# A recommender's phase change reordered: exponent and gates ahead of copies, block tests on GpSimd, late sums shared anew, one step's attention weights by TensorE

## The chip, the cores and the metric

The kernel runs on one core of one Trainium2 chip. The metric is the device time of one execution in microseconds (us). Before the change it is 1994.08 us, the median of 3 runs (1992.85 to 1997.23). The engines are named as the profile names them: PE is TensorE (PEld its weight loads), DVE is VectorE, ACT is ScalarE, POOL is GpSimd, and SP issues most of the DMAs.

## The reference, cut to what matters

For 1024 samples with a history of 100 steps and 128 features, in float32:

```python
# first recurrence (GRU) over the history
r, z = sigmoid(...), sigmoid(...)
n = tanh(i_n + r * h_n)
h = (1 - z) * n + z * h                     # keys[t] = h
# attention scores: an MLP over [keys, q, keys - q, q * keys]; softmax over the 100 steps
attn = softmax(where(mask == 1, score, -inf))
pooled = einsum('bt,btd->bd', attn, keys)   # 1024 x 128
att_seq = pooled.T[:T]                      # step t of the next recurrence uses feature t of pooled
# second recurrence over the keys, from h = 0
r, u = sigmoid([h, x_t] @ Wr.T + br), sigmoid([h, x_t] @ Wu.T + bu)
h_hat = tanh([h * r, x_t] @ Wh.T + bh)
u = att_seq[t][:, None] * u
h = (1 - u) * h + u * h_hat
# the state at the sample's last step, and four other features, go through a last MLP
```

Two things matter here. The weight of step t is column t of `pooled`, so the second recurrence can only begin when the softmax over all 100 steps and the sums over the last keys are done. And the second recurrence runs on samples sorted by length, so that fewer and fewer columns stay alive.

## The kernel before

The 1024 samples stand as two halves of 512 columns, with 128 features on the partitions. `gru_phase` runs the first recurrence: in each of 100 turns TensorE computes both halves' gates and, for the step before, the score MLP (`attend` issues its products, `take` its relus and sends the score rows through a DMA into tiles called s_b). A softmax runs in blocks of 8 to 3 steps: `late_scores` and `late_tops` on VectorE bring the scores into place and take off their maximum, `exponents` runs on ScalarE, and `late_sums` finishes the weights. `Half.pool` multiplies keys by weights and adds them into `pooled`: L713 rescales the old sum, L723 multiplies, L724 adds. `augru_phase` runs the second recurrence.

Everything is issued in an order that is written by hand; each engine takes its own instructions strictly in that order and waits by semaphores. There is no scheduler.

The change is in the passage between the two phases, from `take(T - 2)` to the first steps of `augru_phase`. What stands there before the change:

- `features(g)`: eight groups of four products that begin the last MLP, each into one of two PSUM banks (called f); ScalarE copies each group out (L774), and only then is a bank free for the group after next.
- `where_equal`: an equality test on ScalarE, made of Square (L1083) and Relu (L1084). Four such tests are needed: two on the tiles called block, two on the halves of q0.
- `gate` and `activate`: step 0 of the second recurrence, which has no old state: two products for each half (L1136) and a tanh and a sigmoid for each (L1143).
- The weights of steps 0 to 3 are computed apart from the rest, since the phase needs them first: VectorE sums the first four features (the slice `soon`) of all keys (L733, L1174, L1177) into first_w (L1181); TensorE brings these into the sorted order (L1193), VectorE masks them with block into s_b (L1195), and TensorE adds up groups of partitions (L1198 for step 0, L1208 for a row of each of the four steps). The four rows go through DRAM (att_d) and come back spread over all partitions, by one load for each half and step (L1221 for steps 1 and 2).
- The late sums: the other 28 features (the slice `rest`) of the last seven keys. GpSimd sums all of half 0's last but one block, then half 1's; VectorE sums half 0's last block, one key between the products of step 0, the rest behind them.
- `store_pooled` writes `pooled` to DRAM by eight stores (L1230); `gather_weights` fetches it back in sorted order by eight indirect DMAs of GpSimd (L165); VectorE masks it (L1272) and TensorE transposes it (L1279) in step 2 and 3, for the weights of steps 4 to 99.

PSUM has eight banks. In the passage six of them are the tiles `b[0]` to `b[5]`, shared out by the dictionary `banks` among softmax (e), score transposes (pt), sums (kw) and features (f); `LATE_BANKS` and `NEXT_BANKS` say which of them the first gates of the second phase take, in the order in which they come free.

## Time and profile before

| | before |
|---|---|
| median of 3 runs | 1994.08 us (1992.85 to 1997.23) |
| the profiled execution | 1990.86 us |
| its span, first to last instruction | 1989.1 us |
| ScalarE busy, 1390 to 1400 us | 6.98 of 10 us |
| VectorE busy, 1400 to 1410 us | 5.99 of 10 us |
| GpSimd busy, 1400 to 1410 us | 9.61 of 10 us |
| TensorE's idle time between 1430 and 1440 us | 1.05 us |

A row of an engine's timeline has its start and its length in us, the engine, the line of the kernel, the operation, output and inputs, their shapes and the count of instructions merged into it. In square brackets stands how long the engine had been idle just before, and what released it. The chain of work that ended last goes back from the last instruction to whatever released it, step by step. The times of the timeline are counted from the start of the span; the score MLP's last products end at about 1389 us, and the second phase's own gates begin at 1410.69.

### The profile page before, as it was taken

The page shows a single profiled execution, that of the slowest core. Times are in us where ns is not written, and L with a number is a line of the kernel's source. Part 1 is how long each engine was busy: PE and PEld are TensorE (multiplying, and loading weights), DVE is VectorE, ACT ScalarE, POOL GpSimd, SP SyncE. Part 2 cuts the span into 40 slices and gives each one's busy share as a digit, 9 for nine tenths or more (in the row PEclk, how much of TensorE's full clock was granted, in tenths as well). Part 3 has the DMA queues.
Part 4 walks back from the last instruction along what each step waited for, and adds up shares of the span by engine and source line. Part 5 has one row for each costly group of instructions (what it writes and reads, how often), then busy time and mean ns, then how long its engine had stood idle before and what let it go on. Part 6 is the DMA issues. An engine that isn't in the chain of part 4 may idle for free.

```text
span 1989.1 us, 40757 instructions
## 1 busy us (share of the span) xinstructions
PE 1969.7 (99%) x15252; PEld 919.1 (46%) x15252; DVE 1667.6 (84%) x3010; ACT 935.8 (47%) x1681; POOL 1241.9 (62%) x1283
## 2 busy tenths in 40 slices
PE   9999999999999999999999999999899999999998
PEld 2333333333333333333333333443444556678997
DVE  7888899898979898888889888998677778888995
ACT  4444454454544444444445454445343444445553
POOL 1324759676896959588795948797653454445331
PEclk9999999999999999999999999999999999999999
DMA  4453333223333434356743333332543333333331
GB/s 116 109 111 105 104 107 101 88 86 108 117 100 116 117 101 116 106 152 188 210 151 98 102 104 97 108 96 94 161 139 92 96 111 96 93 103 99 83 82 33
DMA packets 245171, 218.57 MB, mean 110 GB/s; under 512 B 45639, under 2 KB 206900, under 8 KB 244196
## 3 DMA queue, kind: packets, MB, share of 16 engines
q1 hardware_dynamic: 233476, 183.30, 33.0%
q0 software_dynamic: 11200, 32.04, 5.6%
q8 instruction: 122, 2.00, 0.4%
q14 instruction: 85, 0.70, 0.1%
q10 hardware_dynamic: 288, 0.52, 0.1%
HBM read 153.45 MB, written 60.72 MB: 108 GB/s over the span
## 4 chain that ended last, share of the span: by engine, by line
PE 94%; DVE 2%; POOL 1%; DMA 1%; ACT 1%; issue 1%; SPq 0%; another core or an unknown queue 0%; DVEq 0%; ACTq 0%; POOLq 0%
PE ps L612 50%; PE pm L798 17%; PE ph L1329 4%; PE pu L1329 4%; PE pr L1329 4%; PE pr L1325 4%; PE pu L1325 4%; PE ph L1325 4%; POOL pooled L724 1%; POOL kw L723 1%; PE pr L1405 0%; PE ph L1405 0%; DMA item<-att_d 0%; SPq L1230 0%; PE p L1527 0%
## 5 line engine op out<-in xcount | busy, mean ns | idle before, releaser
L612 PE MATMUL ps<-x,wih 128*32 128x512 f32 x4800 | 834.9, 593 | 0.0
L612 PE MATMUL ps<-hn,whh 128*32 128x512 f32 x4752 | 829.0, 592 | 0.0
L612 PEld LDWEIGHTS ps<-x,wih 128*32 128x32 f32 x4800 | 237.2, 110 | 324.4 <-issue 311.6
L612 PEld LDWEIGHTS ps<-hn,whh 128*32 128x32 f32 x4752 | 235.2, 110 | 320.2 <-issue 312.4
L624 ACT ACTIVATE r<-ps,brz 128x512 f32<-128x512 f32 x200 | 137.6, 688 | 380.2 <-PE ps L612 379.9
L597 POOL TENSOR_TENSOR xm<-x,m 128x512 f32<-128x512 f32 x200 | 234.3, 1172 | 83.6 <-DMA m<-mask_d 83.2
L798 PE MATMUL pm<-kq,wkq 128*32 128x512 f32 x1188 | 270.0, 592 | 0.0
L798 PE MATMUL pm<-hn,wk 128*32 128x512 f32 x1188 | 269.9, 592 | 0.0
L598 POOL TENSOR_TENSOR hist<-hist,xm 128x512 f32<-128x512 f32 x200 | 258.9, 1295 | 15.7
L724 POOL TENSOR_TENSOR pooled<-pooled,kw 128x512 f32<-128x512 f32 (+1 forms) x195 | 250.3, 1284 | 15.3
L798 PE MATMUL pm<-mv,w 128*32 128x512 f32 x790 | 252.7, 592 | 2.9 <-DVE e L939 2.9
L723 POOL TENSOR_TENSOR kw<-kt,e 128x512 f32<-128x512 f32 (+1 forms) x195 | 210.0, 1077 | 71.7 <-DVE e L956 71.7
L645 ACT ACTIVATE ps<-ps,bih 128x512 f32<-128x512 f32 x198 | 131.1, 662 | 224.9 <-DVE ps L642 224.0
L208 POOL DMA_INDIRECT rows<-keys_d,idx_k x186 | 182.1, 979 | 73.3 <-POOL rows L207 70.0
L1337 ACT ACTIVATE c<-ph,bh 128x510 f32<-128x510 f32 (+57 forms) x174 | 88.3, 507 | 252.7 <-PE ph L1329 252.6
L632 DVE SCALAR_TENSOR_TENSOR u<-ps,bhh,r 128x512 f32<-128x512 f32 x198 | 147.5, 745 | 69.7 <-PE ps L612 63.9
L655 DVE TENSOR_TENSOR d<-hn,ps 128x512 f32<-128x512 f32 x198 | 136.1, 687 | 36.0 <-ACT ps L645 35.7
L207 POOL COPY rows<-rest 128x1 f32<-128x1 f32 x186 | 35.3, 190 | 199.5 <-DVE rest L1365 177.2
L656 DVE TENSOR_TENSOR d<-ps,d 128x512 f32<-128x512 f32 x198 | 136.9, 691 | 27.0 <-ACT ps L646 12.8
L664 ACT COPY hn<-ps 128x512 f32<-128x512 f32 x198 | 115.4, 583 | 91.8 <-DVE kq L659 91.8
L642 DVE TENSOR_TENSOR ps<-ps,u 128x512 f32<-128x512 f32 x200 | 140.0, 700 | 21.9 <-PE ps L612 0.9
L1357 DVE TENSOR_TENSOR pu<-pu,c 128x510 f32<-128x510 f32 (+57 forms) x173 | 81.9, 473 | 75.0 <-ACT c L1337 72.8
(286 smaller groups left out, 3154.3 us busy)
## 6 DMA issues: line engine op xcount, KB each, us to landing
x<-in_hist_x SPq DMA_DIRECT2D x210, 256.0 KB
keys_d<-kt SPq DMA_DIRECT2D x44, 1024.0 KB
m<-mask_d SPq DMA_DIRECT2D x200, 128.0 KB
wide_d<-kt SPq DMA_DIRECT2D x24, 256.0 KB
sorted_d<-sort SPq DMA_DIRECT2D x32, 192.0 KB
rows<-sorted_d SPq DMA_DIRECT2D x6, 1024.0 KB
s_b<-mv SPq DMA_DIRECT2D x200, 8.0 KB
rows<-keys_d,idx_k POOLq DMA_INDIRECT x186, 2.9
```

The costliest lines, as they stand in the source:

```text
L208: nc.gpsimd.indirect_dma_start(out=r[:, k, :], out_offset=None, in_=keys_d[q], in_offset=bass.IndirectOffsetOnAxis(ap=idx_k[:, k, i : i + ...
L597: nc.gpsimd.tensor_mul(d, x, m)
L598: nc.gpsimd.tensor_add(acc, acc, d)
L612: nc.tensor.matmul(p[ts(q, R), :], lhsT=w[:, g, ts(q, R)], rhs=v, start=(j == 0), stop=(j == len(parts) - 1),)
L624: nc.scalar.activation(r, pr, AF.Sigmoid, bias=brz[:, 0:1])
L632: nc.vector.scalar_tensor_tensor(out=u, in0=ph, scalar=bhh[:, 2:3], in1=r, op0=ALU.add, op1=ALU.mult,)
L642: nc.vector.tensor_add(pi, pi, u)
L723: eng.tensor_mul(d, k, w)
L724: eng.tensor_add(acc, acc, d)
L798: nc.tensor.matmul(p[i][s, :], lhsT=w[:, s], rhs=v, start=start, stop=stop)
L1325: nc.tensor.matmul(p, lhsT=m[:, 1, :], rhs=k, start=True, stop=False)
L1329: nc.tensor.matmul(p, lhsT=m[:, 0, :], rhs=v, start=False, stop=True)
```

## The change

- ScalarE's tests of block (two of the four) become one GpSimd instruction each (add and is_equal, L1104 of the changed kernel), ahead of the sums.
- Features 3 go ahead of half 0's gates; the test of half 0's q0 and the tanh follow; the exponent goes ahead of the copies of features 4 to 7, and half 1's gates go into the banks of pt, ahead of features 6 and 7 instead of behind them.
- Of half 1's last but one block VectorE now sums the rescale and two keys of `rest`, ahead of the last block's scores; GpSimd keeps two. In exchange GpSimd takes two of the three keys of half 0's last block; VectorE keeps one, now behind step 0's products.
- The first sums go into a PSUM tile (first_sums) and are copied to `pooled` afterwards; first_w reads them there.
- Step 0's two products of state and update move from ahead of the maskings to between them.
- The weight of step 1 for half 0 comes from a product of TensorE (at1) instead of a load; the load for half 0 is gone. The sigmoid of that step's update gate goes to SBUF (into item).
- `store_pooled` stores half 1 first. The banks change places.

The order of the instructions on three engines. **TensorE**, behind the last products of the score MLP (pm), before the change; ph and pu are half 0's gates of step 0, `last` the bank of features:

```order
L798 MATMUL pm<-mv,w_0_135 32x512
L798 MATMUL pm<-mv,w_late 32x512
L1136 MATMUL ph<-h_all,wh 128x512
L1136 MATMUL pu<-h_all,wu 128x512
L766 MATMUL last<-m_9180,user 128x200
```

And with the change:

```order
L798 MATMUL pm<-mv,w_0_135 32x512
L798 MATMUL pm<-mv,w_late 32x512
L766 MATMUL last<-m_9180,user 128x200
L766 MATMUL last<-m_9180,item 128x200
L766 MATMUL last<-m_9180,hist 128x200
L766 MATMUL last<-m_9180,cross 128x200
L1143 MATMUL ph<-h_all,wh 128x512
L1143 MATMUL pu<-h_all,wu 128x512
```

One group of features now stands between the score MLP's last products and the gates that reuse its banks.

**ScalarE**, from the second relu of the last scores (mv) on, before the change; L953 is the exponent, L774 a copy of features, L1143 a gate's tanh or sigmoid:

```order
L865 ACTIVATE mv<-pm,bm_147 32x512
L1083 ACTIVATE block<-block,low 128x512
L1084 ACTIVATE block<-block 128x512
L774 COPY part<-last 128x200
L1143 ACTIVATE h_all<-ph,bh 128x512
L774 COPY part<-last 128x200
L1083 ACTIVATE q_160<-q_160,low 128x512
L1084 ACTIVATE q_160<-q_160 128x512
L953 ACTIVATE last<-last 128x32x4
L1156 ACT_TABLE_LOAD
L1156 ACTIVATE table<-table 128x1
L1143 ACTIVATE pu<-pu,bu 128x512
```

And with the change (L1150 is now the tanh or sigmoid):

```order
L865 ACTIVATE mv<-pm,bm_147 32x512
L774 COPY part<-last 128x200
L1083 ACTIVATE q_160<-q_160,low 128x512
L1084 ACTIVATE q_160<-q_160 128x512
L1150 ACTIVATE h_all<-ph,bh 128x512
L1083 ACTIVATE q_160<-q_160,low 128x512
L1084 ACTIVATE q_160<-q_160 128x512
L953 ACTIVATE last<-last 128x32x4
L774 COPY part<-last 128x200
L1163 ACT_TABLE_LOAD
L1163 ACTIVATE table<-table 128x1
L1150 ACTIVATE pu<-pu,bu 128x512
```

The test of block is gone, both tests of q0 stand ahead of the exponent, and a copy stands behind it.

**VectorE**, from first_w to the late sums, before the change:

```order
L1181 TENSOR_TENSOR first_w<-pooled,used 128x128
L975 COPY e<-last 128x32x5
L1189 TENSOR_TENSOR h_all<-h_all,pu 128x512
L1189 TENSOR_TENSOR h_all<-h_all,last 128x512
L713 TENSOR_TENSOR pooled<-pooled,last 128x16x28
L723 TENSOR_TENSOR last<-kt,last 128x16x28
L724 TENSOR_TENSOR pooled<-pooled,last 128x16x28
L1195 TENSOR_TENSOR s_b_156<-last,block 128x512
L1195 TENSOR_TENSOR s_b_158<-last,block 128x512
L1205 TENSOR_TENSOR h_all<-first,h_all 128x512 x2
```

And with the change:

```order
L1189 TENSOR_TENSOR first_w<-last,used 128x128
L975 COPY e<-last 128x32x5
L1193 COPY pooled<-last 128x32x4
L1199 TENSOR_TENSOR h_all<-h_all,pu 128x512
L1201 TENSOR_TENSOR s_b_156<-last,block 128x512
L1199 TENSOR_TENSOR h_all<-h_all,last 128x512
L1201 TENSOR_TENSOR s_b_158<-last,block 128x512
L1211 TENSOR_TENSOR h_all<-first,h_all 128x512 x2
L713 TENSOR_TENSOR pooled<-pooled,last 128x16x28
L723 TENSOR_TENSOR last<-kt,last 128x16x28
L724 TENSOR_TENSOR pooled<-pooled,last 128x16x28
```

The late sums of half 0 move behind step 0's products, and each s_b follows its own half's product.

The diff:

```diff
@@ -75,7 +75,7 @@
 WIDTHS = [[max(LEAST, n) for n in alive] for alive in ALIVE]
 
 FREE = 134 * 256
-LATE_BANKS, NEXT_BANKS = (1, 0, 5), (2, 6, 3, 4)
+LATE_BANKS, NEXT_BANKS = (2, 0, 1), (6, 5, 3, 4)
 
 PR = P // NH
 BQ = B // (P // R)
@@ -1099,7 +1099,9 @@
         take(T - 2)
         halves[1].keep()
         nc.scalar.activation(table, table, AF.Exp)
-        where_equal(later["block", 0], low[:, 1:2])
+        for half in halves:
+            block = later["block", half.i]
+            nc.gpsimd.tensor_scalar(block, block, low[:, 1:2], 0.0, ALU.add, ALU.is_equal)
         some(0)
         attend(T - 1, [b[0], b[1]])
         for half in halves:
@@ -1121,12 +1123,17 @@
         halves[0].pool(T, nc.gpsimd)
         late_1 = list(halves[1].todo)
         halves[1].pool(T, nc.vector, soon)
+        halves[1].todo = late_1
+        halves[1].pool(2, nc.vector, rest)
+        halves[1].pool(T, nc.gpsimd, rest)
         attend(T)
         take(T)
         some(2)
         attend(T + 1)
         some(2)
         take(T + 1)
+        some(3)
+        some(3)
         for half in halves:
             half.store((T - 1) // G)
         gates = []
@@ -1144,24 +1151,24 @@
             return to
 
         gate(halves[0], [pa.tile([P, HB], F32, tag="a", name=f"p{n}") for n in "hu"])
-        where_equal(later["block", 1], low[:, 1:2])
-        some(3)
-        some(3)
+        where_equal(q0[:, ts(0, HB)], low[:, 0:1])
         activate()
         some(4)
-        some(4)
-        where_equal(q0[:, ts(0, HB)], low[:, 0:1])
+        where_equal(q0[:, ts(1, HB)], low[:, 0:1])
         stage(2)
         exponents()
+        some(4)
+        some(5)
+        gate(halves[1], banks["pt"])
         nc.scalar.activation(table, table, AF.Sigmoid)
         update = [activate()]
-        for g in range(5, 2 * GH):
-            some(g)
-            some(g)
-        where_equal(q0[:, ts(1, HB)], low[:, 0:1])
-        gate(halves[1], banks["f"])
+        some(6)
+        some(5)
         activate()
         update.append(activate())
+        some(7)
+        some(6)
+        some(7)
 
         stage()
         e = soft["e"][1]
@@ -1174,23 +1181,22 @@
         nc.vector.tensor_mul(
             d[:, :, 0], pooled[:, :, soon], e[:, :, 0:1].to_broadcast([P, NK, SOON])
         )
+        first_sums = b[0][:, HB - NK * SOON :].rearrange("p (k c) -> p k c", c=SOON)
         nc.vector.tensor_reduce(
-            pooled[:, :, soon], d.rearrange("p k n c -> p k c n"), AX.X, ALU.add
+            first_sums, d.rearrange("p k n c -> p k c n"), AX.X, ALU.add
         )
         w = wp.tile([P, HB], F32, tag="d", name="first_w")[:, : SOON * NK]
         nc.vector.tensor_mul(
-            w.rearrange("p (k c) -> p k c", c=SOON), pooled[:, :, soon], later["used"]
+            w.rearrange("p (k c) -> p k c", c=SOON), first_sums, later["used"]
         )
         weights_to_sbuf()
-        halves[1].todo = late_1 + halves[1].todo
+        nc.vector.tensor_copy(pooled[:, :, soon], first_sums)
         halves[1].pool(T, nc.gpsimd, rest)
 
-        for i in range(NH):
-            nc.vector.tensor_mul(h3[i], h3[i], update[i])
-        halves[0].pool(1, nc.vector, rest)
-        chosen = []
-        for half, p in zip(halves, banks["pt"]):
+        later["chosen"] = chosen = []
+        for half, p in zip(halves, (b[3], b[2])):
             nc.tensor.matmul(p, lhsT=w, rhs=q0[:, half.cols], start=True, stop=True)
+            nc.vector.tensor_mul(h3[half.i], h3[half.i], update[half.i])
             chosen.append(s_bs[NH * (soft["j"] % 2) + half.i])
             nc.vector.tensor_mul(chosen[-1], p, later["block", half.i])
         for half in halves:
@@ -1203,7 +1209,7 @@
                 stop=True,
             )
             nc.vector.tensor_mul(h3[half.i], p, h3[half.i])
-        p = banks["pt"][0]
+        p = b[3]
         for half in halves:
             nc.tensor.matmul(
                 p[ts(half.i, R), :], lhsT=quad, rhs=chosen[half.i], start=True, stop=True
@@ -1215,16 +1221,17 @@
                 out=att_d[i][:SOON], in_=soon_rows[i * R : i * R + SOON, :]
             )
         for t in range(1, 3):
-            for half in halves:
+            for half in halves[2 - t :]:
                 at = item[:, half.cols] if t == 1 else s_bs[NH * ((soft["j"] - 1) % 2) + half.i]
                 later["att", t, half.i] = at
                 nc.sync.dma_start(out=at, in_=att_d[half.i][t].partition_broadcast(P))
-        halves[0].pool(T, nc.vector, rest)
+        halves[0].pool(1, nc.vector, rest)
+        halves[0].pool(T, nc.gpsimd, rest)
         later["halves"] = halves
 
     def store_pooled():
 
-        for half in later["halves"]:
+        for half in reversed(later["halves"]):
             to = pooled_d[half.cols, :].rearrange("(k r) f -> r k f", r=R)
             for p in range(P // R):
                 nc.sync.dma_start(
@@ -1348,10 +1355,22 @@
             if (t, i) == (1, 0):
                 open_gates(1, 0, ("pu",), LATE_BANKS[1:])
             pu = close_gate(t, i, "pu", wu, h)
+            if (t, i) == (1, 0):
+                att[1, 0] = pa.tile([P, HB], F32, tag="a", name="at1")
+                nc.tensor.matmul(
+                    att[1, 0],
+                    lhsT=quad[:, 1:2].to_broadcast([P, P]),
+                    rhs=later["chosen"][0],
+                    start=True,
+                    stop=True,
+                )
             if t == 1:
                 open_gates(1, i, ("ph",), (None, LATE_BANKS[2])[1 - i :])
             nc.scalar.activation(pr, pr, AF.Sigmoid, bias=later["br"])
-            nc.scalar.activation(pu, pu, AF.Sigmoid, bias=later["bu"])
+            u = item[:, :w] if (t, i) == (1, 0) else pu
+            nc.scalar.activation(u, pu, AF.Sigmoid, bias=later["bu"])
+            if (t, i) == (1, 0):
+                pu = att[t, i][:, :w]
             state = states.pop(1 - i, None)
             if state is not None:
                 nc.vector.tensor_mul(state[0], state[0], state[1])
@@ -1359,7 +1378,7 @@
             nc.vector.tensor_mul(r, h, pr)
             if state is not None:
                 nc.vector.tensor_sub(state[3], state[0], state[2])
-            nc.vector.tensor_mul(pu, pu, att.pop((t, i))[:, :w])
+            nc.vector.tensor_mul(pu, u, att.pop((t, i))[:, :w])
             rest = wp.tile([P, HB], F32, name="rest")[:, :w]
 
             nc.vector.scalar_tensor_tensor(
@@ -1607,7 +1626,7 @@
             for i in range(NH):
                 keys[t, i] = later["key", t, i]
                 if t < G - 1:
-                    att[t, i] = later["att", t, i]
+                    att[t, i] = later.get(("att", t, i))
                 else:
                     load_att(t, i)
         open_gates(1, 0, ("pr",), LATE_BANKS)
```

## The prediction

> **What bounds the kernel now.** I read the page first, then the busy time by stretch, then the engines in order of time between 1378 and 1434 us (all instants are us from the start of the span).
>
> ```profile
> span 1989.1 us, 40757 instructions
> PE 1969.7 (99%) x15252; PEld 919.1 (46%) x15252; DVE 1667.6 (84%) x3010; ACT 935.8 (47%) x1681; POOL 1241.9 (62%) x1283
> ...
> 1390.00:1400.00 10.00, 8.52 (x44) 7.25 (x44) 5.63 (x16) 6.98 (x14) 9.69 (x10) 1.00 0.80 233
> 1400.00:1410.00 10.00, 7.34 (x16) 2.79 (x16) 5.99 (x11) 2.82 (x5) 9.61 (x10) 0.83 0.19 62
> 1405.90:1409.20 3.30, 2.80 (x4) 1.17 (x4) 1.73 (x3) 0.00 (x0) 3.14 (x4) 0.50 0.00 0
> 1440.00:1950.00 510.00, 509.37 (x2094) 355.41 (x2094) 421.92 (x1022) 244.46 (x539) 234.01 (x399) 1.00 0.37 99
> ```
>
> TensorE is busy for 99% of the span, so the kernel is as long as TensorE's queue plus TensorE's stops. The columns of the stretches are: length, busy PE, PEld, DVE, ACT, POOL, granted clock, DMA. The phase change is the weak place: between 1390 and 1410 TensorE is idle for 4.1 us, and from 1405.9 to 1409.2 its granted clock is 0.50. Behind it the second phase is full again (509.37 of 510), so what is won here goes through to the end. TensorE's own rows name the stops:
>
> ```profile
> 1389.81 1.12 PE L1136 MATMUL ph<-h_all,wh 128*128 128x512 f32 x2 [0.76 <-ACT mv L865]
> 1391.63 0.50 PE L766 MATMUL last<-m,user 128*128 128x200 f32 x2
> 1392.99 0.50 PE L766 MATMUL last<-m,user 128*128 128x200 f32 x2
> 1398.68 0.61 PE L766 MATMUL last<-m,user 128*128 128x200 f32 x2 [1.48 <-ACT part L774]
> 1401.00 1.02 PE L1136 MATMUL last<-h_all,wu 128*128 128x512 f32 x2
> 1401.86 1.88 PE L1193 MATMUL last<-q,first_w 128*128 128x512 f32 x4
> 1406.40 3.38 PE L1198 MATMUL first<-s_b,quad 128*128 128x512 f32 x4 [2.66 <-DVE s_b L1195]
> 1409.71 1.05 PE L1208 MATMUL last<-s_b,quad 128*32 128x512 f32 x4
> 1433.84 0.64 PE L1279 MATMUL pw<-ident,att_r 128*96 128x128 f32 x4 [0.63 <-DVE att_r L1272]
> ```
>
> Three stops: 0.76, 1.48 and 2.66 us. One group of features takes 1392.99 - 1391.63 = 1.36 us, one 128x512 product 1401.86 - 1401.00 = 0.86. The two products of L1198 (four records) should take 1.72 and took 1409.71 - 1406.40 = 3.31: **1.59 us lost to the half clock** that followed the longest stop. The stop of 1.48 left the clock at 1.00. Together 0.76 + 1.48 + 2.66 + 1.59 = 6.49 us are to be had.
>
> [...]
>
> **The change, part by part.** *Stop 1.* Features 3 now stand ahead of half 0's gates. ScalarE's relus (below) end as before, and 1.36 us of products cover the 0.76. Won: 0.76.
>
> *Stop 2 and the exponent.* ScalarE's rows of before:
>
> ```profile
> 1389.08 1.38 ACT L865 ACTIVATE mv<-pm,bm 32x512 f32<-32x512 f32 x2 [0.65 <-PE pm L798]
> 1394.76 0.72 ACT L1083 ACTIVATE q<-q,low 128x512 f32<-128x512 f32 x1
> 1396.06 0.26 ACT L953 ACTIVATE last<-last 128x128 f32<-128x128 f32 x1
> 1396.33 1.28 ACT L1156 ACT_TABLE_LOAD   x1
> 1398.31 0.55 ACT L774 COPY part<-last 128x200 f32<-128x200 f32 x2
> ```
>
> An equality test costs 1396.06 - 1394.76 = 1.30 here. Two of the four leave for GpSimd, and the exponent moves ahead. From 1390.46 on (the end of the two relus) ScalarE now has a copy (0.3, half of the 0.55), a test, a tanh (0.7, as one of the two relus) and a test: 1390.46 + 0.3 + 1.3 + 0.7 + 1.3 = 1394.1. VectorE decides when the exponent can start:
>
> ```profile
> 1388.82 0.18 DVE L899 COPY last<-top 128x32 f32<-128x32 f32 x1
> 1391.69 1.47 DVE L905 STREAM_TRANSPOSE last<-s_b 128x512 f32<-128x512 f32 x2 [2.69 <-DMA s_b<-mv]
> 1393.86 0.30 DVE L912 TENSOR_TENSOR last<-last,top 128x128 f32<-128x128 f32 x1
> 1396.35 0.27 DVE L920 TENSOR_TENSOR last<-last,on 128x96 f32<-128x96 f32 x1 [2.19 <-ACT last L953]
> 1398.79 0.30 DVE L1174 TENSOR_TENSOR last<-pooled,last 128x128 f32<-128x128 f32 x1
> 1399.84 0.86 DVE L1181 TENSOR_TENSOR first_w<-pooled,used 128x128 f32<-128x128 f32 x1
> 1403.94 0.61 DVE L713 TENSOR_TENSOR pooled<-pooled,last 128x448 f32<-128x448 f32 x1
> 1405.66 1.28 DVE L1195 TENSOR_TENSOR s_b<-last,block 128x512 f32<-128x512 f32 x2
> 1410.42 0.62 DVE L723 TENSOR_TENSOR last<-kt,last 128x448 f32<-128x448 f32 x1
> 1411.73 0.63 DVE L723 TENSOR_TENSOR last<-kt,last 128x448 f32<-128x448 f32 x1
> ```
>
> Into the wait of 2.69 us the change puts half 1's rescale and two of its late sums: 1405.66 - 1403.94 = 1.72 with one sum, 1411.73 - 1410.42 = 1.31 for the second, 3.03 in all. They run from 1388.8 to 1391.85, so the transposes start at 1392.0, 0.3 later. The scores, less their maximum, are ready at 1394.16 + 0.3 = 1394.5; the exponent starts then instead of at 1396.06. ScalarE's copies that release TensorE's banks follow at once, or 2.3 us later behind table load, sigmoid and copy (about 1397.3). TensorE, without its stops, stands at 1389.05 + 1.36 + 1.72 + 2.72 + 1.72 = 1396.6 when it wants the first bank and at 1397.9 for the second. Won: 1.48.
>
> *Stop 3 and the clock.* The sum of step 0's weights waits for GpSimd's four sums of half 0:
>
> ```profile
> 1386.90 1.07 POOL L713 TENSOR_TENSOR pooled<-pooled,e 128x512 f32<-128x512 f32 x1 [6.27 <-DVE e L975]
> 1397.45 0.97 POOL L713 TENSOR_TENSOR pooled<-pooled,e 128x448 f32<-128x448 f32 x1
> 1407.12 0.97 POOL L713 TENSOR_TENSOR pooled<-pooled,e 128x448 f32<-128x448 f32 x1
> 1413.37 1.15 POOL L724 TENSOR_TENSOR pooled<-pooled,kw 128x448 f32<-128x448 f32 x1
> L1583 POOL TENSOR_SCALAR places<-places,own 128x256 f32<-128x256 f32 x1 | 0.9, 941 | 0.1
> ```
>
> After the exponent, VectorE comes to the product of L1174 at 1394.8 + (1398.79 - 1396.35) = 1397.24, and half 0's sums end by 1397.45, when the next piece starts: a wait of some 0.2 us, on the edge. first_w starts 1.05 later (1399.84 - 1398.79), at 1398.5. Its price was 0.86; the same size from PSUM (L1174) took 0.30. It now reads its sums from PSUM, so I take 0.30 (ends 1398.8) and keep 0.86 (1399.4) as the other end. [...] TensorE reaches this point at 1389.05 + 5 x 1.36 + 4 x 0.86 = 1399.3, so it waits for at most 0.1. Its two products end at 1401.0. VectorE meanwhile has two small copies (0.3 each by L1174's size) and then, for each half, one product and one s_b, 0.64 each (half of 1.28), with no late sums (1.72) among them: from 1399.4 on, s_b of half 0 is ready at 1400.7, of half 1 at 1402.0. TensorE's first product of L1198's kind runs from 1401.0 to 1401.9 and the second waits for 0.1 to 0.6, by first_w's price; I take 0.3. A stop of that length keeps the clock. Won: 2.66 + 1.59 - 0.3 = 3.95.
>
> *Block tests on GpSimd.* Two tests of 512 columns; 256 columns took 0.94 with one operation, so 0.94 to 1.9 each, from below, and I take 1.9 (twice the columns). Two are 3.8 us and lie in the 6.27 us in which GpSimd waited: cost nothing, up to 3.1 us each.
>
> *Step 1 by TensorE.* One more 128x512 product in TensorE's dense part: 0.86, in full. It spares one broadcast load and VectorE's wait for it, which had not stopped TensorE.
>
> *Late sums, stores, gather.* Behind stop 3, the next thing that TensorE can wait for is the transpose of the gathered weights at 1433.84:
>
> ```profile
> 1432.42 0.69 DVE L1365 SCALAR_TENSOR_TENSOR rest<-pu,h_all 128x506 f32<-128x506 f32 x1
> 1433.22 0.56 DVE L1272 TENSOR_TENSOR att_r<-att_r,used_s 128x384 f32<-128x384 f32 x1
> ...
> 1415.83 7.66 SPq L1230 DMA_DIRECT2D pooled_d<-pooled  x8
> ...
> 1413.49 4.78 DMA item<-att_d
> 1429.74 3.36 DMA att_r<-pooled_d,idx
> ```
>
> GpSimd had 1397.45 - 1386.90 = 10.55 (half 0), 1407.12 - 1397.45 = 9.67 and 1414.52 - 1407.12 = 7.40 (half 1) us of sums; the rescale and two of the four sums of the middle piece go to VectorE, and two sums of half 0's last piece come instead (4.4), so it ends at 1413.6, 0.9 before its 1414.52. What counts is SP: the eight stores stood behind six broadcast loads (1413.49, 4.78 us), though the sums were done at 1414.52. The loads now come 6.2 us earlier and are five; half 1's stores can go at 1409.3 and only half 0's four wait for 1413.6. At 0.5 to 0.7 each they are out by 1416.2 instead of 1423.5: 7 us earlier, and the gather with them. TensorE gets there 6.2 - 0.86 = 5.3 earlier, so the gather (landed at 1433.10, just before VectorE's mask) keeps ahead by some 1.5 us. Of the stop of 0.63 about 0.1 goes, since the mask still stands behind VectorE's rest.
>
> **The sum.** 0.76 + 1.48 + 3.95 - 0.86 + 0.1 = 5.4 us won. The profiled execution took 1990.86 (span 1989.1 and 1.8 around it), which would become 1985.4. The median of the three runs shown is 1994.08, 3.2 above the profiled one; on that scale the forecast is 1994.08 - 5.4 = **1988.7**. About 0.2% (4.0 us) is what a measurement of this kernel can tell from no change, so the forecast is only just outside it.
>
> **Rivals.** *The gather becomes the wait* (chance 0.13). If the eight stores still take 7.66 us from the moment the last sum is done, they end at 1421.3, 2.2 earlier than before; TensorE then stands at the transpose for 3.1 us more, and a stop of that length halved the clock before. Won: 2.2, or 0.6 with another 1.59 lost: 1991.9 to 1993.5. For it: the last piece of sums ends only 0.9 us earlier. Against it: the slow issues stood beside loads that now end earlier.
>
> *VectorE's new sums hold the exponent* (0.09). If the two sums placed at 1388.8 cost what GpSimd's do (0.97 + 2 x 2.2 = 5.4 instead of 3.03), scores, exponent and first_w are 2.4 later; TensorE idles for 1.9. Won: 3.5, or 1.9 if the clock falls: 1990.6 to 1992.2. Against it: the same instructions, from PSUM, are in the rows above.
>
> *Slower: the block tests hold GpSimd* (0.04). Half 0's sums start when the tests end, and the sum of step 0's weights already waits for them on the edge, so each us over 6.27 is a us of TensorE, and from about 2.5 us on the half clock is back. It decides from 4.2 us over, 5.2 us a test. At 7.5 a test it is 8.7 over: 8.7 - 0.4 + 1.59 - 5.4 = 4.5 slower, 1998.6. For it: no test of this size on GpSimd is in the trace. Against it: 0.94 for half the columns.
>
> *More is won* (0.06): first_w at 0.30 and no stop left, 6.3 us, 1987.8.
>
> **How the numbers follow.** The forecast has 0.68. Its own range is 1986.7 to 1990.7, two us to each side, about half the spread of the three runs before (1992.85 to 1997.23). Taking in the gather and the held exponent gives 1985.5 to 1992.8 with some 2 in 10 outside. A win of 5.4 shows as over 0.2% in about five of six measurements: 0.68 x 0.83 + 0.06 + a little of the held exponent = 0.64 faster; slower 0.05 from the block tests and chance; 0.31 within 0.2%.
>
> **What would show it.** Right: no row of TensorE between 1389 and 1405 with more than 0.5 us of idling, granted clock 1.00 throughout, the products of L1198's kind at 0.86 each; the exponent on ScalarE near 1394.5; first_w near 0.30; both block tests done by 1386.9; the products that follow them on TensorE near 1403.5 (1409.71 before); the last store issued near 1416. Wrong: a wait of several us before the transposes of the gathered weights, GpSimd's first sum of half 0 later than 1387, or the clock at 0.50 anywhere in this stretch.

## The result and the profile after

| | before | after |
|---|---|---|
| median of 7 runs each, side by side | 1994.55 us (1992.85 to 1997.23) | 1988.49 us (1985.91 to 1990.21) |
| the profiled execution | 1990.86 us | 1985.99 us |
| its span | 1989.1 us | 1984.2 us |
| ScalarE busy, 1390 to 1400 us | 6.98 of 10 us | 7.48 |
| VectorE busy, 1400 to 1410 us | 5.99 of 10 us | 6.16 |

The changed kernel is faster: after to before 0.9967 (95% interval 0.9955 to 0.9978), 6.06 us by the medians and 4.87 us by the two profiled executions.

From the page after and from its busy time by stretch, with the columns of the prediction (length, busy PE, PEld, DVE, ACT, POOL, granted clock, DMA share, GB/s):

```profile
span 1984.2 us, 40759 instructions
PE 1969.6 (99%) x15254; PEld 921.9 (46%) x15254; DVE 1667.0 (84%) x3012; ACT 932.7 (47%) x1677; POOL 1242.7 (63%) x1284
...
1390.00:1400.00 10.00, 10.00 (x44) 7.25 (x43) 8.18 (x24) 7.48 (x15) 9.61 (x10) 1.00 0.92 266
1400.00:1410.00 10.00, 9.93 (x24) 3.76 (x25) 6.16 (x10) 1.92 (x3) 9.61 (x10) 1.00 0.34 104
1440.00:1950.00 510.00, 507.52 (x2103) 355.59 (x2102) 420.36 (x1027) 242.90 (x540) 230.01 (x393) 1.00 0.36 98
```

TensorE's 4.1 idle us between 1390 and 1410 have shrunk to 0.07, and the clock stays at 1.00. But the second phase, 509.37 busy us of 510 before, now shows 507.52: something was lost behind the stretch that the change is about, and the experiments have to say whether the change lost it.

TensorE's own rows after, from the timeline (start, length, engine, line, operation, shapes; the idle time ahead in square brackets). L1198 is the product with first_w, L1204 the sum for step 0, L1214 the rows for the four steps, L1360 the new product of step 1, L1286 the transposes pw:

```profile
1398.07 1.88 PE L1198 MATMUL last<-q,first_w 128*128 128x512 f32 x4
1399.87 2.32 PE L1204 MATMUL first<-s_b,quad 128*128 128x512 f32 x4
1402.13 1.05 PE L1214 MATMUL last<-s_b,quad 128*32 128x512 f32 x4
...
1406.64 1.02 PE L1360 MATMUL at<-s_b,quad 128*128 128x512 f32 x2
...
1426.90 0.64 PE L1286 MATMUL pw<-ident,att_r 128*96 128x128 f32 x4 [0.42 <-DVE att_r L1279]
1433.16 0.61 PE L1286 MATMUL pw<-ident,att_r 128*96 128x128 f32 x4 [0.51 <-PE pu L1332]
```

No row between the score MLP and pw carries a wait any more. One wait is hidden in a merged row: the four records of L1204 take 2.26 us to the start of the next row, the four of L1198 ahead of them 1.80.

The rows of ScalarE's exponent, VectorE's first_w and GpSimd's first gather after:

```profile
1393.03 0.26 ACT L953 ACTIVATE last<-last 128x128 f32<-128x128 f32 x1
1397.36 0.29 DVE L1189 TENSOR_TENSOR first_w<-last,used 128x128 f32<-128x128 f32 x1
1417.35 1.05 POOL L165 DMA_INDIRECT att_r<-pooled_d,idx  x1 [5.05 <-DMA pooled_d<-pooled]
```

The instants of two executions can't be compared as they stand, since the first 1378 us differ by up to 2 us from run to run (the copy below starts between 1377.87 and 1379.82 in the fourteen profiles). I therefore count from VectorE's copy L899, the last one ahead of all that was changed, in each trace:

```profile
1377.87 0.18 DVE L899 COPY last<-top 128x32 f32<-128x32 f32 x1
```

It started at 1379.09 in the profile before. **The stretch from L899 to the first pw** was 1433.84 - 1379.09 = 54.75 us and is 1426.90 - 1377.87 = 49.03 us: 5.72 us won. Where it was won, by starts of TensorE's rows, in us after L899:

| TensorE's row | before | after | won in this piece |
|---|---|---|---|
| product with first_w | 22.77 | 20.20 | 2.57 |
| first sum for step 0 | 27.31 | 22.00 | 2.74 |
| rows of the four steps | 30.62 | 24.26 | 1.05 |
| pw | 54.75 | 49.03 | -0.64 |

The last piece holds the new product of step 1 (0.86 us more) and a shorter wait at pw (0.63 before, 0.42 after).

In the one repeat of the changed kernel (last experiment) these starts came out within 0.1 us, so single steps of 0.3 us and more can be judged by them, where medians with a spread of 4 us cannot.

### The profile page after: what moved, and what is told of

It reads as the page before. It is cut to its first block, busy times and chain, and to the rows that moved or that the text cites. A ratio compares the mean times of both kernels' runs of the same rounds, so it can differ in the third digit from the quotient of the medians.

```text
span 1984.2 us, 40759 instructions
## 1 busy us (share of the span) xinstructions
PE 1969.6 (99%) x15254; PEld 921.9 (46%) x15254; DVE 1667.0 (84%) x3012; ACT 932.7 (47%) x1677; POOL 1242.7 (63%) x1284
## 4 chain that ended last, share of the span: by engine, by line
PE 95%; DVE 3%; issue 1%; ACT 1%; DVEq 0%; ACTq 0%
PE ps L612 50%; PE pm L798 17%; PE ph L1336 4%; PE pr L1336 4%; PE pu L1336 4%; PE pr L1332 4%; PE pu L1332 4%; PE ph L1332 4%; PE last L766 1%; PE pr L1424 0%; PE ph L1424 0%; DVE pu L1381 0%; DVE ps L657 0%; DVE d L656 0%; DVE pu L1376 0%
## 5 line engine op out<-in xcount | busy, mean ns | idle before, releaser
L612 PE MATMUL ps<-x,wih 128*32 128x512 f32 x4800 | 812.5, 592 | 0.0
L612 PE MATMUL ps<-hn,whh 128*32 128x512 f32 x4752 | 806.9, 592 | 0.0
L798 PE MATMUL pm<-hn,wk 128*32 128x512 f32 x1188 | 264.4, 592 | 0.0
L798 PE MATMUL pm<-kq,wkq 128*32 128x512 f32 x1188 | 264.4, 592 | 0.0
L798 PE MATMUL pm<-mv,w 128*32 128x512 f32 x790 | 247.4, 593 | 2.0 <-DVE e L939 2.0
L657 DVE TENSOR_TENSOR ps<-ps,d 128x512 f32<-128x512 f32 x198 | 138.5, 699 | 6.7
```

The lines of the kernel that those rows point to most:

```text
L612: nc.tensor.matmul(p[ts(q, R), :], lhsT=w[:, g, ts(q, R)], rhs=v, start=(j == 0), stop=(j == len(parts) - 1),)
L657: nc.vector.tensor_add(pi, pi, d)
L798: nc.tensor.matmul(p[i][s, :], lhsT=w[:, s], rhs=v, start=start, stop=stop)
```

## The experiments

My theory: the win is TensorE's three stops and the half clock, less the new product, and the gather keeps ahead. The rivals are those of the prediction: the gather hard behind, the exponent, GpSimd's tests. Each kernel below is the changed one with one part undone, except the first, which is the kernel before with one thing added. The measure is the stretch from L899 to pw, 49.03 us in the changed kernel.

| kernel | L899 to pw, us | against the changed kernel |
|---|---|---|
| before | 54.75 | +5.72 |
| before_filler | 53.12 | +4.09 |
| order_before | 51.62 | +2.59 |
| features_behind | 49.84 | +0.81 |
| sums_ahead | 50.24 | +1.21 |
| tests_act | 49.48 | +0.45 |
| tests_x3 | 56.39 | +7.36 |
| sums_sbuf | 49.73 | +0.70 |
| sums_shared_before | 49.11 | +0.08 |
| stores_before | 49.52 | +0.49 |
| step1_load | 48.17 | -0.86 |
| pair_and_load | 49.14 | +0.11 |
| after_again | 49.10 | +0.07 |

**The half clock by itself** (before_filler): the kernel before, and TensorE kept busy through its longest stop.

```diff
             nc.vector.tensor_mul(chosen[-1], p, later["block", half.i])
+        for _ in range(3):
+            nc.tensor.matmul(
+                b[2], lhsT=later["wh"][:, 1, :], rhs=q0[:, :HB], start=True, stop=True
+            )
```

> The kernel before, with three products of 512 columns (3 x 0.86 = 2.58 us, into a bank that nobody reads) where TensorE stopped for 2.66 us. They start when the weights' products end, so the next products can start when they did. If the half clock is the price of that stop: the granted clock stays at 1.00, the four records of L1198's kind take 1.72 instead of 3.31 us, and the stretch from VectorE's copy L899 (the last before 1380 us) to the first transposes pw takes 54.75 - 1.6 = 53.15 us. Rival, the clock falls for another reason (the load of the whole passage): still 0.50 there, stretch 54.75. Rival, the gather follows hard behind: clock at 1.00, but 1 us or more of new waiting at pw, stretch 54.2 or more.

TensorE's rows of this kernel (L1197 the filler, L1202 and L1212 the sums that were L1198 and L1208; `<-issue` stands where the profile shows nothing that was waited for):

```profile
1402.56 2.74 PE L1197 MATMUL last<-q,wh 128*128 128x512 f32 x6
1405.38 1.98 PE L1202 MATMUL first<-s_b,quad 128*128 128x512 f32 x4
1407.30 1.05 PE L1212 MATMUL last<-s_b,quad 128*32 128x512 f32 x4
...
1431.22 0.64 PE L1283 MATMUL pw<-ident,att_r 128*96 128x128 f32 x4 [0.42 <-issue]
```

The sums start when they did (27.28 us after L899, 27.31 before), but their four records take 1407.30 - 1405.38 = 1.92 us instead of 3.31, and 1.63 us of the stretch are gone, with useless work. So 1.4 us of the win is the clock alone; the other 0.2 is the idle time at pw, 0.42 instead of 0.63.

Two stretches of 1 us of the kernel before (the columns again) give the same size in another way:

```profile
1405.00:1406.00 1.00, 0.00 (x0) 0.00 (x0) 0.97 (x3) 0.00 (x0) 0.92 (x2) 0.92 0.00 0
1409.00:1410.00 1.00, 1.00 (x4) 0.14 (x4) 0.39 (x2) 0.00 (x0) 0.92 (x2) 0.88 0.00 0
```

Mean clocks of 0.92 and 0.88 put the half clock from about 1405.84 to 1409.24, 3.4 us. TensorE worked from 1406.40 on, and half of the 2.84 us up to 1409.24 is 1.42. The record has one profile of the kernel before; whether its clock falls here in every execution is not shown.

**The order of gates, copies and exponent** (order_before): the passage between the last scores and the last sums as before, without block's test.

```diff
-        some(3)
-        some(3)
...
         gate(halves[0], [pa.tile([P, HB], F32, tag="a", name=f"p{n}") for n in "hu"])
-        where_equal(q0[:, ts(0, HB)], low[:, 0:1])
+        some(3)
+        some(3)
         activate()
         some(4)
-        where_equal(q0[:, ts(1, HB)], low[:, 0:1])
+        some(4)
+        where_equal(q0[:, ts(0, HB)], low[:, 0:1])
         stage(2)
         exponents()
...
-        gate(halves[1], banks["pt"])
+        gate(halves[1], banks["f"])
```

> The changed kernel with gates, copies of features, q0's tests and the exponent in the order of before (block tests on GpSimd, the sums, s_b and step 1's product stay as changed). ScalarE's copies wait for TensorE's features there, so the exponent starts 17.0 us after L899 again (15.2 in the changed kernel), and two stops of TensorE come back, 0.76 and 1.48 us; what follows is as in the changed kernel. Stretch from L899 to pw 49.03 + 2.2 to 2.6 = 51.3 to 51.6 us, the clock stays at 1.00. Rival, the exponent is early without the new order, since a test of block is gone from ScalarE: only the 0.76 returns, 49.8 us. Rival, the stops of before add up to a half clock here: 53 us.

```profile
1389.88 1.13 PE L1141 MATMUL ph<-h_all,wh 128*128 128x512 f32 x2 [0.72 <-ACT mv L865]
...
1396.77 0.50 PE L766 MATMUL last<-m,cross 128*128 128x200 f32 x2
1398.75 0.61 PE L766 MATMUL last<-m,user 128*128 128x200 f32 x2 [1.48 <-ACT part L774]
1399.19 0.50 PE L766 MATMUL last<-m,item 128*128 128x200 f32 x2
```

Both stops return, with the exponent 17.0 us after L899 again, though a test is gone from ScalarE: TensorE's features, not ScalarE's load, set it in that order. These TensorE rows also show why a stop costs more than its brackets. Rows of this kind start 0.34 us apart in the dense parts. Around the stop they start 1398.75 - 1396.77 = 1.98 apart, and the next 1399.19 - 1398.75 = 0.44: 1.74 us lost, where the brackets say 1.48. Of the 0.26 between, 0.16 is the row's own length (the brackets count from the end of a row, 0.50 us after its start, and dense rows start 0.34 apart), and 0.10 is the slower first row behind the stop.

**Stop 1 alone** (features_behind): features 3 behind half 0's gates, their copy behind the tanh.

```diff
-        some(3)
-        some(3)
...
+        some(3)
         where_equal(q0[:, ts(0, HB)], low[:, 0:1])
         activate()
+        some(3)
```

> The changed kernel with features 3 behind half 0's gates again, their copy behind the tanh. TensorE stops for 0.76 us ahead of the gates. The exponent comes 0.4 us later, which lies in VectorE's wait of 0.62 us for GpSimd's sums. Stretch 49.03 + 0.76 = 49.8 us. Rival, the stop is absorbed by a later wait (the 0.46 us between the two sums of step 0's weights): 49.3 us.

0.81 us, as expected; the wait was not absorbed later. The exponent starts 15.60 us after L899, 0.44 later than in the changed kernel, and VectorE's wait for GpSimd falls from 0.62 to 0.21: that lateness was hidden as expected.

**VectorE's late sum ahead of s_b** (sums_ahead).

```diff
+        halves[0].pool(1, nc.vector, rest)
         later["chosen"] = chosen = []
...
-        halves[0].pool(1, nc.vector, rest)
         halves[0].pool(T, nc.gpsimd, rest)
```

> The changed kernel with VectorE's one late sum of half 0 (rescale, product, sum: about 1.9 us) ahead of s_b, as it stood before. VectorE idles for 0.46 us there, so s_b comes some 1.4 us later and TensorE stops for that before it adds up groups of partitions. If the clock falls by the stop's length, 1.4 to 1.9 us leave it at 1.00, as the 1.48 us of before did: stretch from L899 to pw 49.03 + 1.4 to 1.9 = 50.4 to 50.9 us. Rival, any stop at this place halves the clock: 52.0 us or more.

```profile
1402.06 2.32 PE L1205 MATMUL first<-s_b,quad 128*128 128x512 f32 x4 [1.09 <-DVE s_b L1202]
1404.31 1.05 PE L1215 MATMUL last<-s_b,quad 128*32 128x512 f32 x4
```

The stop is 1.09 us, where I had expected 1.4 to 1.9; the stretch is 1.21 us longer, and the granted clock stays at 1.00 (1400 to 1408 us): the four records take 2.25 us as in the changed kernel. So the rival, that any stop at this place halves the clock, does not hold in this run. That the length decides is not shown either (last experiment).

The late sum gives back 1.09 us of stop 3, not 2.66. In the kernel before, VectorE did something else ahead of s_b:

```profile
1403.33 0.69 DVE L1189 TENSOR_TENSOR h_all<-h_all,last 128x512 f32<-128x512 f32 x1 [1.80 <-ACT last L1143]
```

It waited 1.80 us for ScalarE's last gate of half 1, for a product that the first s_b did not need. With the change that gate comes earlier and the product stands behind the first s_b. No run put the product back in front, so this share of the win is read from the rows and not tested.

**Block's tests** (tests_act, tests_x3): back on ScalarE; and three times on GpSimd.

```diff
-        for half in halves:
-            block = later["block", half.i]
-            nc.gpsimd.tensor_scalar(block, block, low[:, 1:2], 0.0, ALU.add, ALU.is_equal)
+        where_equal(later["block", 0], low[:, 1:2])
...
+        where_equal(later["block", 1], low[:, 1:2])
         where_equal(q0[:, ts(0, HB)], low[:, 0:1])
```

> The changed kernel with the two tests of block back on ScalarE, the first where it was before, the second ahead of q0's first test. ScalarE and VectorE are both ready for the exponent at 1393.0 in the changed kernel, so a test of 1.3 us more makes the exponent 1.3 us later; 0.6 of it lies in VectorE's wait for GpSimd's sums, and TensorE has 0.4 to spare: stretch from L899 to pw 49.03 + 0.3 to 0.9 = 49.3 to 49.9 us. Rival, the tests' place is what the new order hangs on (the copies that release TensorE's banks come late too): 50.3 us or more. Rival, ScalarE had the time: 49.0 us.

```diff
             block = later["block", half.i]
+            for _ in range(2):
+                spare = wp.tile([P, HB], F32, tag="kw", name="spare")
+                nc.gpsimd.tensor_scalar(
+                    spare, block, low[:, 1:2], 0.0, ALU.add, ALU.is_equal
+                )
             nc.gpsimd.tensor_scalar(block, block, low[:, 1:2], 0.0, ALU.add, ALU.is_equal)
```

> The changed kernel with three tests of each block on GpSimd instead of one (four more, of 2.0 us each: 8.0; the results of the added ones are not used). GpSimd was idle for 2.24 us in front of half 0's sums, and VectorE already waited 0.62 us for them, so the sums end 5.8 us later and first_w too. TensorE had 0.4 us to spare there: it stops for about 5.3 us ahead of the weights' products or between these and the sums, and the clock halves behind it (up to 1.6 us more). Stretch from L899 to pw: 49.03 + 5.3 + 0 to 1.6 = 54.3 to 55.9 us, about the kernel before. Rival, the sums of step 0's weights don't hang on GpSimd on the edge: less than 2 us of it shows.

On ScalarE they make the exponent 1.15 us later (16.31 after L899 instead of 15.16) and cost 0.45 us. On GpSimd they are free because of this gap, in the changed kernel:

```profile
1379.40 4.01 POOL L1104 TENSOR_SCALAR block<-block,low 128x512 f32<-128x512 f32 x2
1385.65 1.08 POOL L713 TENSOR_TENSOR pooled<-pooled,e 128x512 f32<-128x512 f32 x1 [2.24 <-DVE e L975]
```

With six tests the gap is overrun. TensorE's rows of tests_x3, and its stretch behind the stop (columns as above):

```profile
1404.99 3.75 PE L1203 MATMUL last<-q,first_w 128*128 128x512 f32 x4 [5.29 <-issue]
1408.54 2.47 PE L1209 MATMUL first<-s_b,quad 128*128 128x512 f32 x4
...
1404.00:1409.00 5.00, 4.01 (x5) 1.80 (x6) 3.38 (x8) 0.00 (x0) 4.76 (x6) 0.50 0.00 0
```

The stop is 5.29 us (expected 5.3), and four records that take 1.80 us at full clock take 1408.54 - 1404.99 = 3.55: 1.75 more. The stretch, 56.39 us, is half a us over the expected range and 1.64 us longer than before.

**first_w's inputs** (sums_sbuf): the sums in SBUF, as before.

```diff
-        first_sums = b[0][:, HB - NK * SOON :].rearrange("p (k c) -> p k c", c=SOON)
+        first_sums = pooled[:, :, soon]
...
-        nc.vector.tensor_copy(pooled[:, :, soon], first_sums)
```

> The changed kernel with the first sums in SBUF again, without the copy. If it is two operands in SBUF that made first_w 0.86 us while GpSimd works, first_w takes 0.8 to 0.9 us again (0.29 in the changed kernel), ends 0.6 us later, and with the 0.4 us that TensorE had to spare it costs 0.2 us: stretch 49.2 us. Rival, its size before was chance or came from what stood beside it then: first_w 0.3 us, stretch 49.0 us.

Rows of VectorE and of GpSimd in this kernel:

```profile
1397.72 1.20 DVE L1189 TENSOR_TENSOR first_w<-pooled,used 128x128 f32<-128x128 f32 x1
...
1397.63 1.14 POOL L724 TENSOR_TENSOR pooled<-pooled,kw 128x448 f32<-128x448 f32 x1
1398.73 1.02 POOL L723 TENSOR_TENSOR kw<-kt,e 128x448 f32<-128x448 f32 x1
```

first_w takes 1.20 us, more than I had expected, and its stop costs TensorE 0.70. It starts just after a sum of GpSimd has started and ends at 1398.92, 0.15 us behind that sum's end (1398.77); GpSimd's next product takes 1.02 instead of 0.97. In the kernel before it ended at 1400.70, 0.14 behind GpSimd's sum from 1399.42 (1.14 long). So the price is not a fixed 0.86: in both places first_w lasts for the rest of GpSimd's instruction and 0.14 to 0.15 us more. No run left GpSimd idle beside it.

**The sharing of the late sums and the order of the stores** (sums_shared_before, stores_before).

```diff
-        halves[1].todo = late_1
-        halves[1].pool(2, nc.vector, rest)
-        halves[1].pool(T, nc.gpsimd, rest)
...
+        halves[1].todo = late_1 + halves[1].todo
         halves[1].pool(T, nc.gpsimd, rest)
...
         halves[0].pool(1, nc.vector, rest)
-        halves[0].pool(T, nc.gpsimd, rest)
+        halves[0].pool(T, nc.vector, rest)
...
-        for half in reversed(later["halves"]):
+        for half in later["halves"]:
```

> The changed kernel with the late sums shared as before (GpSimd all of half 1's, VectorE the rest of half 0's behind step 0's products) and half 0 stored first. If the new sharing and order pay only by keeping the gather ahead: GpSimd's last sum ends 1.2 (offset) earlier than before's 1414.52, at about 1413.5, the stores of half 1 wait for it, the last is issued near 1417 to 1420 instead of 1414.8, and the transposes pw wait for 1 to 4 us; the clock may halve there. Stretch 50 to 53 us. VectorE's scores start 0.3 earlier. Rival, the gather was never close: no wait over 0.6 at pw, stretch 49.0 or a little less.

The second kernel has the last pair of these lines alone:

> The changed kernel with half 0's four stores of the pooled sums ahead of half 1's, as before, and the late sums shared in the new way. GpSimd's last sum, of half 0, ends 34.4 us after L899 and then holds all eight stores: at 0.85 us each the last is issued 41 us after L899 (36.9 in the changed kernel), and the first gather starts 43 to 44 us after it (39.5). The gather had about 1.5 us to spare, so the mask waits and TensorE stops at pw for 2 to 3 us. Stretch 51 to 52 us. Rival, the order of the stores is indifferent, as the sharing of the sums was: 49.0 us.

Both expectations were wrong, the first altogether. With the old sharing the first gather starts 1419.42 - 1379.82 = 39.60 us after L899 (L899 stood at 1379.82 there), in the changed kernel 1417.35 - 1377.87 = 39.48: no difference, and the stretch is 0.08 longer. With the old order of stores alone, all eight wait for GpSimd's last sum. SP's row and VectorE's mask of that kernel (L899 at 1379.04):

```profile
1413.56 4.11 SPq L1237 DMA_DIRECT2D pooled_d<-pooled  x8
...
1427.94 0.56 DVE L1279 TENSOR_TENSOR att_r<-att_r,used_s 128x384 f32<-128x384 f32 x1 [0.33 <-issue]
1428.56 0.64 PE L1286 MATMUL pw<-ident,att_r 128*96 128x128 f32 x4 [0.85 <-issue]
```

Issued together, the stores take 0.51 us each, not the 0.85 I had counted. The gather starts at 40.88, 1.40 late; the mask waits 0.33 (the profile names no releaser; I take it for the gather) and TensorE 0.43 more than in the changed kernel. So in that run the gather had about 1.1 us to spare, not 2 to 3 too few.

**Step 1's weights loaded again, and a further step** (step1_load, pair_and_load). The first undoes TensorE's product; the second also puts the two maskings next to each other, since TensorE lost 2.26 - 1.80 = 0.46 us between the two sums for step 0.

```diff
-            for half in halves[2 - t :]:
+            for half in halves:
...
-                att[1, 0] = pa.tile([P, HB], F32, tag="a", name="at1")
-                nc.tensor.matmul(
...
```

> The changed kernel with step 1's weights of half 0 loaded again instead of TensorE's product. If the product costs its 0.86 us in full and the load comes in time or is hidden: stretch from L899 to pw 49.03 - 0.86 = 48.2 us, and the time 0.9 us less than the changed kernel (not to be told apart by the times alone). Rival, the load comes late: VectorE waits for it by 2 us or more at step 1's product of update and weight, and TensorE stops behind it, since the steps are now earlier: stretch 49.0 or more.

```diff
-            nc.vector.tensor_mul(h3[half.i], h3[half.i], update[half.i])
+            if half.i == 0:
+                nc.vector.tensor_mul(h3[0], h3[0], update[0])
             chosen.append(s_bs[NH * (soft["j"] % 2) + half.i])
             nc.vector.tensor_mul(chosen[-1], p, later["block", half.i])
+        nc.vector.tensor_mul(h3[1], h3[1], update[1])
```

> The changed kernel with step 1's weights of half 0 loaded (48.17 us from L899 to pw in the run of that alone) and VectorE's two maskings into s_b next to each other, half 1's product of state and update behind them. TensorE lost 0.46 us between the two sums of step 0's weights, since that product of 0.6 us stood in front of the second s_b. If it was this, the four records of the sums take 1.8 us instead of 2.26, and the stretch is 48.17 - 0.46 = 47.7 us. Rival, the late product delays the state and TensorE waits at step 1: 48.2 us or more. As a time it is 1.3 us less than the changed kernel, too little to be told apart by the medians.

Without the product, pw comes 0.86 us earlier, exactly its length. VectorE waits 2.33 us for the load, and no stop of TensorE follows. As a time it doesn't show: 1989.16 us (1986.08 to 1989.7, 5 runs; 0.9965 of before, 0.9952 to 0.9979). In pair_and_load the second sum does follow the first (the four records take 1.91 us instead of 2.26), and then the win is lost. The stretch, 49.14 us, lies where the rival had it (48.2 or more), but not for its reason: no row of TensorE shows a stop ahead of pw. GpSimd's last gather for half 0, the mask, and pw, first of step1_load (L899 at 1378.96):

```profile
1423.20 0.94 POOL L165 DMA_INDIRECT att_r<-pooled_d,idx  x1 [0.30 <-issue]
...
1426.53 0.55 DVE L1279 TENSOR_TENSOR att_r<-att_r,used_s 128x384 f32<-128x384 f32 x1
1427.13 0.64 PE L1286 MATMUL pw<-ident,att_r 128*96 128x128 f32 x4 [0.42 <-issue]
```

and then of pair_and_load (L899 at 1379.23):

```profile
1423.20 0.94 POOL L165 DMA_INDIRECT att_r<-pooled_d,idx  x1 [0.30 <-issue]
...
1427.76 0.56 DVE L1281 TENSOR_TENSOR att_r<-att_r,used_s 128x384 f32<-128x384 f32 x1 [1.21 <-issue]
1428.37 0.64 PE L1288 MATMUL pw<-ident,att_r 128*96 128x128 f32 x4 [1.72 <-issue]
```

The mask needs these four gathers. In the first kernel it starts 2.4 us after the last of them was issued (1426.53 - 1424.14), behind VectorE's own work; in the second it waits until 3.6 us after (1427.76 - 1424.14), and TensorE idles 1.30 us more. The profile names no releaser for this wait either; the gathers are what the mask still needs there. Its median, 1987.76 us (1985.6 to 1989.06, 6 runs; 0.9964 of before, 0.9952 to 0.9976), cannot be told from the changed kernel's. In both kernels the load stands ahead of the stores in SP's queue again, and the first gather starts 40.36 and 40.09 us after L899 instead of 39.48. **No version here is shown to beat the changed kernel.** In step1_load the 0.86 us are there in the stretch but not in the medians; in pair_and_load they are given back at the gather. The pairing without the load was not tried.

**The changed kernel once more** (after_again).

> The changed kernel itself. The stretch from L899 to pw repeats within 0.2 us of 49.03; the time from the second pw to the end of the span, 551.0 us in its first profile and between 549.0 and 554.0 in those of other kernels with the same second phase, comes out anywhere in that range if it is a matter of the run, and again near 551 if it belongs to the kernel.

The stretch is 49.10 us, 0.07 off; the median 1987.68 us (1987.06 to 1992.45, 8 runs), 0.9971 of before (0.996 to 0.9981). From the second pw to the end of the span it took 552.3 us, and 551.0 in the first profile. The kernel before took 1989.1 - 1440.09 = 549.0 in its profile, but before_filler, whose second phase is the same code as before's, took 1990.9 - 1437.47 = 553.4, and the other kernels 551.3 to 554.0. The profile before was thus the quickest of all behind pw (it was also 3.7 us below its kernel's median), and that kernel's own second phase, in before_filler, was slower than the changed one's. Nothing says that the 2 us are the change's. Part of the spread is one stop, ahead of the first step that handles both halves at once. It was 1.03 us long before, 1.24 after, and longest in step1_load:

```profile
1947.88 0.57 PE L1412 MATMUL pr<-h_all,wr 128*128 128x140 f32 x2 [3.10 <-DVE h_all L1465]
...
1946.88 0.32 ACT L1344 ACTIVATE c<-ph,bh 128x76 f32<-128x76 f32 x1 [2.64 <-remote]
```

VectorE and TensorE wait there for ScalarE, and ScalarE for something that the profile marks only as remote. What that is was not tried.

Another part is the granted clock behind this stop, and here the length of the stop does not tell whether it falls. Rows of TensorE and stretches of 1 us, of before_filler and of sums_shared_before:

```profile
1951.48 0.78 PE L1409 MATMUL pr<-h_all,wr 128*128 128x140 f32 x2 [1.25 <-issue]
1953.00:1954.00 1.00, 1.00 (x6) 1.00 (x6) 0.75 (x3) 0.11 (x1) 0.00 (x0) 0.50 0.15 52
...
1948.75 0.51 PE L1422 MATMUL pr<-h_all,wr 128*128 128x140 f32 x2 [1.75 <-issue]
1949.00:1950.00 1.00, 0.94 (x8) 0.75 (x7) 0.32 (x2) 0.62 (x2) 0.00 (x0) 1.00 0.57 138
```

After 1.25 us the clock was at 0.50, after 1.75 us it stayed at 1.00. In six of the fourteen profiles it fell there, for 3.4 us each time: before_filler, features_behind, sums_sbuf, stores_before, step1_load and after_again. These six took 552.3 to 554.0 us from the second pw to the end, the other eight, before and after among them, 549.0 to 552.6. The rest of the spread lies ahead of the stop: from the second pw to its beginning it took 509.5 us before, 511.2 after and 512.8 in before_filler, and why is open.

## Why the prediction was right, point by point

The forecast was 1988.7 us and 5.4 us won; the median came out at 1988.49, and the stretch gave 5.72. That the median lies within 0.2 us of the forecast is luck: the same kernel had 1987.68 in the second measurement, and single runs of it lie 4 us apart. The terms in the stretch were off by 0.33, -0.16 and 0.11 us, which also cancels in part.

- *Stop 1 and 2* (0.76 and 1.48): the mechanism held, undone alone they return (features_behind, order_before). The size was a little small: up to the product with first_w 2.57 us were won where 2.24 were forecast, because a stop costs more than its bracket (1.74 for 1.48, order_before). The exponent started 15.16 us after L899; the forecast's 1394.5 is 15.41.
- *Stop 3 and the clock* (2.66 + 1.59 - 0.3 = 3.95): 2.74 + 1.05 = 3.79. The clock's share was oversized: 1.59 compared the half-clock records with dense rows (1.72), but even at full clock these four records take 1.92 (before_filler), so the clock was 3.31 - 1.92 = 1.39. Against the same 1.92 the wait between the two sums that is left is 2.26 - 1.92 = 0.34, and pair_and_load, which took it away, won 0.35; 0.3 was forecast. The prediction also let the clock go by the length of the stop (kept at 0.3, back from about 2.5 us, an estimate from before's stops of 1.48 and 2.66). No run bears that out: it fell after 1.25 us and stayed after 1.75 (last experiment). Why the stop is gone was seen in part only: besides the late sum it was VectorE's 1.80 us of waiting for half 1's gate, which the prediction does not name.
- *first_w* at 0.30: 0.29. That the input in PSUM makes the difference is now shown: undone, it takes 1.20. With both inputs in SBUF it ended 0.15 us behind GpSimd's sum there and 0.14 in the kernel before; with one in PSUM, in the changed kernel, it ran from 1397.36 to 1397.65, inside a sum of GpSimd from 1397.26 to 1398.40.
- *GpSimd's tests* at 1.9 each and free: 2.0 each, with 2.24 us of idle time left. What they buy is 0.45 us (tests_act), which the prediction had not priced by itself. Its slower rival is sized right: by its own sum, tests of 6 us in all for each block would lose 5.73 - 0.4 + 1.59 - 5.4 = 1.5 us against before; six tests of 2 us lost 1.64 in the stretch.
- *Step 1's product*, 0.86 in full: shown to the last digit (step1_load).
- *The gather*: its start moved from 1425.92 - 1379.09 = 46.83 to 39.48 us after L899, 7.35 us earlier, where 7 were forecast. Here the reason given was wrong in part. The new sharing of the sums and the order of the stores were credited with it; sums_shared_before has neither and starts its gather 0.12 us later. What is left is that everything ahead of the stores in SP's queue came earlier, which the prediction named too. The stores' new order matters only together with the new sharing (0.49 us).
- *The rival that the gather becomes the wait* (0.13) did not happen, but it stands close behind. The spare time was put at 1.5 us; stores_before found 1.1, and pair_and_load used it up with 0.86 + 0.35 = 1.2 us of further win and a gather that started 0.6 later.
- *The rival that VectorE's new sums hold the exponent* (0.09) did not happen: the rescale and the two sums took 1390.60 - 1387.55 = 3.05 us (3.03 forecast), not 5.4.
- *The wait at pw*: 0.1 forecast, 0.21 measured. The 0.2 was a wait for the gather: VectorE's mask started 0.80 us after its rest (L1365) before, and 0.60 after (1426.30 - 1425.70). The 0.42 that is left is the mask, as the prediction had it. In every profile here pw starts 0.04 to 0.06 us after the mask's end, and TensorE's weight load names it:

```profile
1426.30 0.55 DVE L1279 TENSOR_TENSOR att_r<-att_r,used_s 128x384 f32<-128x384 f32 x1
1426.90 0.39 PEld L1286 LDWEIGHTS pw<-ident,att_r 128*96 128x96 f32 x4 [1.25 <-DVE att_r L1279]
```

What stays open: why the mask could start 1.2 us earlier in step1_load than in pair_and_load after gathers issued at the same instants, what ScalarE waits for at 1947 us, and what decides whether a stop brings the half clock. None of these was tried.

## What to carry to other kernels

On an engine that is 99% busy, add up its stops in the stretch by the starts of rows, not by the idle time shown, and look at the granted clock behind each of them: a half clock is a cost of its own (1.39 us of four records here), and here the length of the stop did not tell whether it came (it came with 1.25 us and not with 1.75). Work that kept TensorE busy through the stop got it back (3.31 us became 1.92 in before_filler). When several chains run side by side, every gain is worth only as much as the next chain lets through, so measure the slack of the runner-up (by delaying it) before working further on the first. Where medians scatter by more than the edit is worth, compare a stretch between two fixed instructions.

## What the runs showed of the hardware that I had not expected

- The granted clock stayed at 1.00 after stops of 1.09 (sums_ahead), 1.48 (before) and 1.75 us (sums_shared_before) and went to 0.50 with stops of 1.25 (before_filler), 2.66 (before) and 5.29 us (tests_x3). It stayed there for 3.4 us with the stops of 1.25 and 2.66. With the stop of 5.29 it read 0.50 from 1404.00 to 1409.00 and 0.64 in the us behind, at least 5.7 us in all.
- A VectorE instruction of 128x128 with two inputs in SBUF took 0.86 us in one place (before) and 1.20 in another (sums_sbuf), and 0.29 with one input in PSUM (after): in both places with two it ended 0.14 to 0.15 us behind the GpSimd instruction that ran when it started.
- GpSimd's test, one input and two operations, took 2.0 us for 128x512 (4.01 for two, after), nearly twice its product of two inputs of the same size (L713, 1.07 us before).
